# Adding the second mixture's results in the output rows by accumulating scatters, instead of a last pass over two tables

## The chip, the cores and the metric

The kernel runs on one core of a Trainium2 chip. The metric is the device time of the whole kernel in microseconds (us), as a median over runs. PE is the matrix engine (TensorE), ACT ScalarE, DVE VectorE, POOL GpSimd, SP SyncE. SP and ACT issue plain transfers (DMAs); POOL issues indirect ones, which take a list of row numbers (gathers and scatters).

## The reference

Four stages follow one another on 6250 rows (nodes) of 256 features, with 100000 edges: a first graph attention, a first mixture of experts (6 experts, the best two for each row), a second graph attention, and a second mixture of experts. Only the last matters here:

```python
def _L1_ffn_ref(x, Wg, bg, W1, b1, W2, b2):
    xf = x.reshape(-1, D)
    gate_logits = xf @ Wg + bg
    top_w, top_i = jax.lax.top_k(gate_logits, TOP_K)
    top_w = jax.nn.softmax(top_w, axis=-1)
    w_dense = jnp.sum(jax.nn.one_hot(top_i, E, dtype=xf.dtype) * top_w[..., None], axis=1)
    out = jnp.zeros_like(xf)
    for e in range(E):
        h = jax.nn.gelu(xf @ W1[e] + b1[e], approximate=False)
        out = out + w_dense[:, e:e + 1] * (h @ W2[e] + b2[e])
    return out.reshape(B, L, D)
...
x = x + _L1_ffn_ref(_layernorm(x, axis=-1)[None], ...)[0]
```

Each row of the result is the row itself plus the weighted results of two of the eight experts (TOP_K = 2). The hidden size of an expert is 1024.

## The kernel before, in words

Rows are handled in tiles of 128 (NT = 49 tiles, the last one with 106 rows). The class Routed does the bookkeeping of a mixture. For every tile it chooses two experts per row, counts, and gives each (row, expert) pair a slot in a table in DRAM that is grouped by expert (f_rows). POOL scatters the rows there (L768). Whenever 256 slots of one expert are full, they make a block (NB = 256, NTB = 2 tiles of 128). The second mixture plans for 54 blocks. A short block is filled with null rows, whose row numbers lie beyond the last tile.

The function ffn1 (L1421) is the second mixture, interleaved with the second graph attention. Its order of work is written by hand: one loop over steps s (L1520), whose body issues instructions for all five engines, and each engine follows its own queue in that order. seq is the list of the tiles still to be gathered. In a step

- SP loads the next block: its rows xr, its bias columns and its output bias (fetch, L838), the first weights w1 (1 MB, L1453), and for the block before it the second weights w2 (1 MB, fetch2, L1460);
- PE runs the second layer of the block before the last (outer, L1481) and the first layer of the last one (inner, L1470). ACT applies the activation (L1474) and scales the results into buffers named by (L892, four of them, which is two blocks); DVE adds the bias and, for a row's first expert, the row itself (L897, L899);
- POOL gathers the neighbours' rows of one tile for the attention (L1239), with the scatters of the mixture set between the gathers through a list named outbox (L1605). When no gathers are left, the scatters follow one another, each behind a small memset named gap (L1617).

Where a block's result goes: places (L867) works out for each of its rows a row number in a table in DRAM, f1_parts (L640), which has two halves. The first half takes the result of a row's second expert, the other half (at offset part) that of its first; null rows go to places of their own. So every row of the table is written once, and the scatters (send, L902) are declared free of order among each other. While gathers remain (s < len(seq) - 1), the finished blocks aren't scattered at once: SP stores them in a table late_y (L1562). From step len(seq) + 2 on, two of these kept blocks per step are loaded again (fetch_kept, L1513, 256 KB each, three buffers named late) and scattered after the step's own block (L1567-1570). 32 blocks are kept, 22 are scattered directly.

After the loop, rest (L1665) has a loop for blocks that the plan left out; its bounds come from left_i, and for these inputs it has no turn. Then a last pass (L1632-1663) loads both halves of the table, four tiles at a time, on two queues, adds them on DVE (L1658) and stores the sums to the output.

Of the kernel before, what the change touches and what calls it, by code (L numbers as in the profile page):

```python
# [9 lines left out]
F32 = mybir.dt.float32  # L10
# [25 lines left out]
def gnn_moe_kernel(ctx: ExitStack, tc: tile.TileContext, a: dict, out: bass.AP):  # L36
# [587 lines left out]
    class Routed:  # L624
# [4 lines left out]

        def __init__(self, name, n_e, keep_pool, ids, own=False, spare=None):  # L630
            self.name, self.n_e, self.ids, self.own = name, n_e, ids, own
# [6 lines left out]
            self.written_by = []  # L638
            self.part = NT * P + self.n_blocks * NB
            self.parts = dram.tile([2 * self.part, D], F32, name=f"{name}_parts")  # L640
            self.table = dram.tile([n_e * REG + NB, RW], F32, name=f"{name}_rows")
# [225 lines left out]
        def places(self, pool, xr, bcol, j, tok=None):  # L867

            w = pool.tile([P, NTB], F32, name="bw", bufs=4)
            first = pool.tile([P, NTB], F32, name="bfirst", bufs=4)  # L870
            nc.vector.tensor_scalar(first, xr[:, :, C_E0], bcol[:, self.n_c : self.n_c + 1], None, op0=OP.is_equal)
            nc.vector.tensor_mul(w, xr[:, :, C_WD], first)
            nc.vector.tensor_add(w, w, xr[:, :, C_W1])
            if tok is None:
                tok = pool.tile([P, NTB], I32, name="btok", bufs=6)

            off = pool.tile([P, NTB], F32, name="boff", bufs=4)
            nc.vector.tensor_scalar(off, xr[:, :, C_TOK], float(NT * P), float(j * NB), op0=OP.is_ge, op1=OP.mult)
            nc.vector.tensor_add(off, off, xr[:, :, C_TOK])
            nc.vector.scalar_tensor_tensor(tok, first, float(self.part), off, op0=OP.mult, op1=OP.add)  # L880
            return w, tok, first

        def put(self, pool, b, i, py):


            y = self.drawn(pool, b, i, py)
            self.finish(b, i, y)
            return y, b["tok"][:, i : i + 1]

# [11 lines left out]

        def send(self, y, tok):  # L902
            put = nc.gpsimd.indirect_dma_start(  # L903
# [3 lines left out]
            self.apart(put, "parts")  # L907
            tc.add_to_no_dep_group(f"{self.name}parts", put.ins)

        def due(self, n_rows, last):  # L910
# [14 lines left out]
        def left(self, out_i):  # L925

            s = self.short

            nc.vector.tensor_scalar(s[0:1, 0:1], s[0:1, 0:1], -float(self.planned), float(self.planned),
                                    op0=OP.mult, op1=OP.add)  # L930
            nc.vector.tensor_tensor(s[0:1, 1:2], s[0:1, 1:2], s[0:1, 0:1], OP.max)
            nc.vector.tensor_copy(out_i, s)

# [28 lines left out]
    def ffn0(k0, t0_d, a0_d, late, order_pool):  # L962
        NX = a["L0_ffn_expert_w1"].shape[0]
        moe, rw1, rw2, rb1, rb2 = (k0[k] for k in ("moe", "rw1", "rw2", "rb1", "rb2"))
        with tc.tile_pool(name="f0g", bufs=1) as fp, tc.tile_pool(name="f0r", bufs=2) as rp, \
                tc.tile_pool(name="f0w", bufs=4) as wp, tc.tile_pool(name="f0h", bufs=2) as hp, \
                tc.tile_pool(name="g0b", bufs=2) as gp:
            with tc.tile_pool(name="f0p", bufs=2, space=PSUM) as psum:
# [103 lines left out]
                while s < len(pairs) or ready or coming or new or q1 or q2 or q3 or g1 or g2 or g3 or drawn \  # L1072
# [3 lines left out]
                    for b, i, y in drawn:  # L1076
                        moe.finish(b, i, y)
                        results.append(partial(moe.send, y, b["tok"][:, i : i + 1]))
                    drawn = []
# [341 lines left out]
    def ffn1(tab, bias_b):  # L1421
        NX, _, HD = a["L1_ffn_W1"].shape
        NM = HD // P
        with tc.tile_pool(name="f1", bufs=1) as fp, tc.tile_pool(name="f1r", bufs=2) as rp, \
# [9 lines left out]
            list_i = keep.tile([1, 2, P], I32, name="list_i")  # L1434
            left_i = keep.tile([1, 2], I32, name="left_i")
            moe = Routed("f1", NX, fp, node_s, own=True, spare=6 * (NB - 1))
            moe.columns(b1c)
            with tc.tile_pool(name="f1p", bufs=2, space=PSUM) as psum:
# [73 lines left out]

                def fetch_kept(j):  # L1513
                    y = hp.tile([P, NTB, D], F32, name="late", bufs=3)
                    nc.sync.dma_start(y, y_d[j * P : (j + 1) * P])
                    return [partial(moe.send, y[:, i, :], toks[:, j, i : i + 1]) for i in range(NTB)]

                gap = fp.tile([1, 1], F32, name="gap")
                s = 0
                while s < len(seq) or ready or new or cur or prev or q1 or q2 or group or outbox or coming or kept:  # L1520

                    prev, cur = cur, new
                    new = fetch(*ready.pop(0)) if ready else None
                    if cur is not None:
# [33 lines left out]
                    if prev is not None:  # L1558
# [7 lines left out]
                        prev = None  # L1566
                    if s > len(seq) + 1:  # L1567
                        for _ in range(2):
                            if kept:
                                sends += fetch_kept(kept.pop(0))  # L1570
                    if new is not None:
# [59 lines left out]

        with tc.tile_pool(name="f1o", bufs=8) as op_, \  # L1632
                tc.manual_schedule(engines={ET.SP, ET.PE, ET.Activation, ET.DVE, ET.Pool}):
            loads = [(g, min(4, NT - g)) for g in range(0, NT, 4)]
            ys = []

            def load():
                if not loads:
                    return
                g, n = loads.pop(0)  # L1640
                y = op_.tile([P, 2, 4, D], F32, name="yg")
                k = min(n, NFULL - g)
                for c in range(2):
                    r = c * moe.part + g * P
                    eng = nc.sync if c == 0 else nc.scalar
                    if k:
                        eng.dma_start(y[:, c, :k, :], moe.parts[r : r + k * P, :].rearrange("(t p) d -> p t d", p=P))
                    if k < n:
                        eng.dma_start(y[:NTAIL, c, k, :], moe.parts[r + k * P : r + k * P + NTAIL, :])
                ys.append((g, n, k, y))  # L1650

            for _ in range(6):
                load()
            while ys:
                g, n, k, y = ys.pop(0)
                eng = nc.sync if g % 8 else nc.scalar
                if k:
                    nc.vector.tensor_add(y[:, 0, :k, :], y[:, 0, :k, :], y[:, 1, :k, :])  # L1658
                    eng.dma_start(out[g * P : (g + k) * P, :].rearrange("(t p) d -> p t d", p=P), y[:, 0, :k, :])
                if k < n:  # L1660
                    nc.vector.tensor_add(y[:NTAIL, 0, k, :], y[:NTAIL, 0, k, :], y[:NTAIL, 1, k, :])
                    eng.dma_start(out[NFULL * P : N, :], y[:NTAIL, 0, k, :])
                load()

    def rest(moe, list_i, left_i):  # L1665
# [3 lines left out]
        with tc.tile_pool(name="rs", bufs=1) as pool, tc.tile_pool(name="rsp", bufs=1, space=PSUM) as psum:  # L1669
            first = nc.values_load(left_i[0:1, 0:1], min_val=0, max_val=moe.n_blocks)  # L1670
            end = nc.values_load(left_i[0:1, 1:2], min_val=0, max_val=moe.n_blocks)
            with tc.For_i(first, end, 1) as j:
                e = nc.values_load(list_i[0:1, 0, bass.ds(j, 1)], engines=[ET.SP], min_val=0, max_val=NX - 1)
# [18 lines left out]
                tok = pool.tile([P, NTB], I32, name="tok")  # L1692
                nc.vector.scalar_tensor_tensor(tok, first_, float(moe.part), xr[:, :, C_TOK],
                                               op0=OP.mult, op1=OP.add)
                xT = pool.tile([P, 2, NB], F32, name="xT")
# [15 lines left out]
                for i in range(NTB):  # L1711
                    py = psum.tile([P, D], F32, name="py")
                    for m in range(NM):
# [6 lines left out]
                                                   op0=OP.mult, op1=OP.add)  # L1720
                    nc.gpsimd.indirect_dma_start(
                        out=moe.parts[:, :], out_offset=bass.IndirectOffsetOnAxis(ap=tok[:, i : i + 1], axis=0),
                        in_=y, in_offset=None)

# [45 lines left out]
```

## Time and profile before

| | |
|---|---|
| median of 3 runs | 2446.48 us (2446.15 to 2448.04) |
| the profiled execution's own time | 2447.71 us |
| its span (first to last instruction) | 2446.0 us |
| granted PE clock, mean over the span | 0.873 |
| PE busy | 1848.9 us, 76% of the span |
| POOL busy | 1498.5 us, 61% |
| DVE busy, ACT busy | 1222.0 us (50%), 943.2 us (39%) |
| bytes moved | 471.68 MB, 193 GB/s in the mean |
| scatters to f1_parts from late, from by | 64 and 44 |

The page's second part cuts the span into 40 slices of 61.2 us; a digit is the busy share of an engine in a slice, in tenths. A chain of waits follows the work that ended last back to what released it, step by step. A line of a timeline gives the start, the busy time, the engine, the source line, the operation with what it writes and reads, and in brackets the idle time before it with what ended that. "To landing" is the time from the issue of a transfer to the signal that its data has arrived. All source lines in this part of the text are those of the kernel before.

### The profile page before, as it was taken

Reading aid. Unit: us, or ns where it says so; the run is one execution under the profiler, and the core shown is the slowest. Engines: PE = TensorE matmul, PEld = TensorE weight load, DVE = VectorE, ACT = ScalarE, POOL = GpSimd, SP = SyncE. Lnnn points to the kernel's source line nnn. Section 1 sums busy time; section 2 is a strip of 40 time slices with the busy share of each in tenths; the row PEclk is TensorE's granted clock in tenths of the full one; section 3 lists DMA queues with packets and bytes.
Section 4 is the critical chain, followed back from the end, with each engine's and each line's share of the span. In section 5 each row is a group of like instructions: output and inputs, shape, how many; then the busy total and the mean of one; then the engine's idle time right before and its main releaser. Section 6 shows DMA issues by size and latency. Waiting matters only on the chain.

```text
span 2446.0 us, 31094 instructions
## 1 busy us (share of the span) xinstructions
PE 1848.9 (76%) x8343; PEld 1545.0 (63%) x8344; DVE 1222.0 (50%) x4459; ACT 943.2 (39%) x1967; POOL 1498.5 (61%) x1778
## 2 busy tenths in 40 slices
PE   3834757887986455259699999999989797799990
PEld 2622546676774343247588888887778676588880
DVE  3658765653227545365555565655645454311112
ACT  2754445553445421014244444433433332334330
POOL 2556366767637377777777777777777774244420
PEclk8955778998998876679899999999999898899995
DMA  7513354768769644446667767676666665387748
GB/s 215 125 42 118 107 161 134 220 191 243 232 196 299 182 116 109 109 155 188 189 197 245 244 209 243 204 226 222 204 199 204 200 198 157 123 295 258 277 163 314
DMA packets 346251, 471.68 MB, mean 193 GB/s; under 512 B 70205, under 2 KB 283236, under 8 KB 346070
## 3 DMA queue, kind: packets, MB, share of 16 engines
q1 hardware_dynamic: 261868, 272.15, 35.6%
q0 software_dynamic: 72112, 186.44, 25.6%
q10 hardware_dynamic: 12090, 11.03, 1.3%
q8 instruction: 69, 1.13, 0.2%
q14 instruction: 112, 0.92, 0.1%
HBM read 374.44 MB, written 95.02 MB: 192 GB/s over the span
## 4 chain that ended last, share of the span: by engine, by line
PE 38%; POOL 16%; DMA 10%; issue 9%; DVE 7%; ACT 7%; SPq 1%; POOLq 0%; DVEq 0%; ACTq 0%
PE py L1481 10%; PE ph L1470 10%; POOL g L1239 10%; PE sums L1293 7%; PE ph L1038 5%; DMA g<-t_d,idx 4%; POOL f_rows L768 2%; PE py L1048 2%; POOL idx L253 2%; DMA yg<-f_parts 2%; DMA idx<-src_d,start_i 2%; DVE g L1284 1%; ACT L1474 1%; ACT L402 1%; POOL f_parts L903 1%
## 5 line engine op out<-in xcount | busy, mean ns | idle before, releaser
L1239 POOL DMA_INDIRECT g<-t_d,idx x813 | 776.7, 955 | 249.2 <-issue 229.5
L1470 PE MATMUL ph<-bxT,w 128*128 128x256 f32 x1728 | 411.7, 396 | 29.6 <-ACT hT L1474 29.6
L1470 PEld LDWEIGHTS ph<-bxT,w 128*128 128x128 f32 x1728 | 338.2, 199 | 90.5 <-ACT hT L1474 43.0
L1293 PE MATMUL sums<-g,ident 128*128 128x256 f32 x1626 | 386.5, 397 | 3.1 <-DVE g L1284 3.0
L1481 PE MATMUL py<-w,hT 128*128 128x256 f32 x1728 | 384.9, 381 | 0.3 <-DMA w<-in_L_ffn_W 0.3
L1293 PEld LDWEIGHTS sums<-g,ident 128*128 128x128 f32 x1626 | 323.1, 200 | 59.9 <-DVE g L1284 12.5
L1481 PEld LDWEIGHTS py<-w,hT 128*128 128x128 f32 x1728 | 328.3, 191 | 45.1 <-DMA w<-in_L_ffn_W 0.5
L768 POOL DMA_INDIRECT f_rows<-rw,slot x196 | 199.4, 1017 | 91.8 <-issue 45.9
L897 DVE SCALAR_TENSOR_TENSOR by<-ob,bw,by 128x256 f32<-128x256 f32 x216 | 98.0, 481 | 266.9 <-ACT by L892 266.9
L1474 ACT ACTIVATE hT<-ph,bcol 128x256 f32<-128x256 f32 x432 | 177.9, 472 | 137.5 <-PE ph L1470 132.2
L1284 DVE TENSOR_TENSOR g<-g,weights 128x2048 f32<-128x2048 f32 (+6 forms) x88 | 229.6, 2610 | 0.0
L903 POOL DMA_INDIRECT f_parts<-by,btok x108 | 105.5, 977 | 153.1 <-DVE by L897 105.3
L1263 ACT ACT_TABLE_LOAD x36 | 46.2, 1283 | 391.7 <-DVE lg L1262 268.3
L1550 PE MATMUL pT<-ident,xn 128*128 128x128 f32 x98 | 24.5, 341 | 184.8 <-DVE xn L1547 184.8
L892 ACT ACTIVATE by<-py,bw 128x256 f32<-128x256 f32 x216 | 92.5, 473 | 154.9 <-PE py L1481 121.8
L1041 ACT ACTIVATE h<-ph,bcol 128x256 f32<-128x256 f32 x216 | 90.7, 471 | 158.6 <-PE ph L1038 97.8
L903 POOL DMA_INDIRECT f_parts<-by,toks x44 | 42.3, 961 | 161.8 <-DVE by L899 123.2
L1550 PEld LDWEIGHTS pT<-ident,xn 128*128 128x128 f32 x98 | 13.4, 167 | 197.5 <-issue 188.7
L1254 DVE TENSOR_TENSOR lg<-g,own 128x32 f32<-128x32 f32 (+6 forms) x88 | 16.7, 199 | 238.3 <-DMA g<-t_d,idx 211.2
L446 PE MATMUL proj<-we,xT 128*128 128x264 f32 x392 | 107.7, 421 | 27.5 <-ACT xT L462 27.5
L1038 PE MATMUL ph<-bxT,w 128*128 128x256 f32 x432 | 110.6, 412 | 16.0 <-ACT bxT L864 14.9
L1038 PE MATMUL ph<-h,w 128*128 128x256 f32 x432 | 112.8, 420 | 0.6 <-ACT h L1041 0.6
(325 smaller groups left out, 2909.7 us busy)
## 6 DMA issues: line engine op xcount, KB each, us to landing
w<-in_L_ffn_W SPq DMA_DIRECT2D x108, 1024.0 KB
w<-in_L_ffn_expert_w SPq DMA_DIRECT2D x162, 256.0 KB
xr<-f_rows SPq DMA_DIRECT2D x108, 264.0 KB
yg<-f_parts SPq DMA_DIRECT2D x36, 512.0 KB
g<-t_d,idx POOLq DMA_INDIRECT x813, 3.2
late_y<-by SPq DMA_DIRECT2D x64, 128.0 KB
late<-late_y SPq DMA_DIRECT2D x32, 256.0 KB
ob<-in_L_ffn_expert_b SPq DMA_DIRECT2D x54, 128.0 KB
```

The lines of the kernel that those rows point to most:

```text
L446: nc.tensor.matmul(ph, xT[:, k, :], we[:, k, :], start=(k == 0), stop=(k == 1))
L768: put = nc.gpsimd.indirect_dma_start(out=self.table[:, :], out_offset=bass.IndirectOffsetOnAxis(ap=slot[:np_, c, i : i + 1], axis=0), in_= ...
L892: nc.scalar.activation(y, py, AF.Copy, scale=b["w"][:, i : i + 1])
L897: nc.vector.scalar_tensor_tensor(y, b["ob"], w, y, op0=OP.mult, op1=OP.add)
L903: put = nc.gpsimd.indirect_dma_start(out=self.parts[:, :], out_offset=bass.IndirectOffsetOnAxis(ap=tok, axis=0), in_=y, in_offset=None,)
L1038: nc.tensor.matmul(ph[:, m, :], b["ws"][i][:, k, m * P : (m + 1) * P], hi[:, k, :], start=(k == 0), stop=(k == 1))
L1239: nc.gpsimd.indirect_dma_start(out=g[:, k, :], out_offset=None, in_=halves(tab), in_offset=bass.IndirectOffsetOnAxis(ap=idx[:, o : o + 1], ...
L1284: nc.vector.tensor_mul(gv, gv, al[:, k0 : k0 + m, :, None].to_broadcast([P, m, H, C]))
L1293: nc.tensor.matmul(po, ident, g[:, k, :D], start=False, stop=k0 + k == q["K"] - 1)
L1470: nc.tensor.matmul(ph[:, q, :], b["w1"][:, k, m * P : (m + 1) * P], b["xT"][:, k, :], start=(k == 0), stop=(k == 1))
L1474: nc.scalar.activation(hT[:, m, :], ph[:, q, :], AF.Gelu, bias=b["bcol"][:, m : m + 1])
L1481: nc.tensor.matmul(py, b["hT"][:, m, i * P : (i + 1) * P], b["w2"][:, m, :], start=(m == 0), stop=(m == NM - 1))
```

## The change

The second mixture gets the output itself as its table (argument result). The row numbers are the plain ones, and each scatter adds to the output row in place of writing to a row of its own. Null rows have numbers above the last row and are dropped by a bounds check. The output must be zero before the first addition, so SP writes zeros to it, seven tiles at a time, in the first seven steps of ffn1 (clear). Scatters of one block name different rows and are declared free of order among each other; scatters of different blocks are not, so the first of a block waits until those of the block before have landed. Kept blocks are fetched from step len(seq) on, in one load of two blocks, into the buffers of the gathers (g, five of them), and they are scattered ahead of the step's own block. The last pass is removed. rest gets a further loop, with zero or one turn, that clears the output again when the plan was broken. In the changed file the lines of ffn1 and of the steps before it lie up to 32 lines lower; the scatter is L924, the ACT copy into by L897.

```diff
-        def __init__(self, name, n_e, keep_pool, ids, own=False, spare=None):
+        def __init__(self, name, n_e, keep_pool, ids, result=None, own=False, spare=None):
+            self.result = result
...
+            if self.result is not None:
+                nc.vector.tensor_copy(tok, xr[:, :, C_TOK])
+                return w, tok, first
...
-        def send(self, y, tok):
+        def send(self, y, tok, j):
+            if self.result is not None:
+                put = self.added(y, tok)
+                tc.declare_no_dep(put.ins, group=f"{self.name}sum{j}", reason="other rows")
+                tc.add_to_no_dep_group(f"{self.name}sum{j}", put.ins)
+                return
...
+        def added(self, y, tok):
+            return nc.gpsimd.indirect_dma_start(
+                out=self.result[:, :], out_offset=bass.IndirectOffsetOnAxis(ap=tok, axis=0),
+                in_=y, in_offset=None, bounds_check=self.result.shape[0] - 1, oob_is_err=False, compute_op=OP.add,
+            )
...
+    def clear(rows, zero, g, n):
+        k = min(n, rows.shape[0] // P - g)
+        nc.sync.dma_start(rows[g * P : (g + k) * P, :].rearrange("(t p) d -> p t d", p=P),
+                          zero[:, None, :].to_broadcast([P, k, D]))
+        if k < n:
+            nc.sync.dma_start(rows[NFULL * P : N, :], zero[:NTAIL, :])
...
-            moe = Routed("f1", NX, fp, node_s, own=True, spare=6 * (NB - 1))
+            moe = Routed("f1", NX, fp, node_s, out, own=True, spare=6 * (NB - 1))
...
-                def fetch_kept(j):
-                    y = hp.tile([P, NTB, D], F32, name="late", bufs=3)
-                    nc.sync.dma_start(y, y_d[j * P : (j + 1) * P])
-                    return [partial(moe.send, y[:, i, :], toks[:, j, i : i + 1]) for i in range(NTB)]
+                def fetch_kept(js):
+                    g = ap_.tile([P, CH, D + H], F32, name="g", bufs=5)
+                    y = g.rearrange("p k d -> p (k d)")[:, : len(js) * NTB * D].rearrange(
+                        "p (b i d) -> p b i d", i=NTB, d=D)
+                    nc.sync.dma_start(y, y_d[js[0] * P : (js[-1] + 1) * P].rearrange("(b p) i d -> p b i d", p=P))
+                    return [partial(moe.send, y[:, b, i, :], toks[:, j, i : i + 1], j)
+                            for b, j in enumerate(js) for i in range(NTB)]
...
+                    if s < NT // 7:
+                        clear(out, moe.null[:, 0, :D], s * 7, 7)
...
-                    if s > len(seq) + 1:
-                        for _ in range(2):
-                            if kept:
-                                sends += fetch_kept(kept.pop(0))
+                    if s >= len(seq) and kept:
+                        sends = fetch_kept(kept[:2]) + sends
+                        del kept[:2]
...
-        with tc.tile_pool(name="f1o", bufs=8) as op_, \
...
-                if k:
-                    nc.vector.tensor_add(y[:, 0, :k, :], y[:, 0, :k, :], y[:, 1, :k, :])
-                    eng.dma_start(out[g * P : (g + k) * P, :].rearrange("(t p) d -> p t d", p=P), y[:, 0, :k, :])
...
+            again = nc.values_load(left_i[0:1, 2:3], min_val=0, max_val=1)
+            zero = pool.tile([P, D], F32, name="zero_rows")
+            nc.vector.memset(zero, 0.0)
+            with tc.For_i(0, again, 1):
+                for g in range(0, NT, 7):
+                    clear(moe.result, zero, g, 7)
```

More of the change, by code (lines that the diff above doesn't have):

```diff
@@ L638, in __init__ @@
             self.written_by = []
-            self.part = NT * P + self.n_blocks * NB
-            self.parts = dram.tile([2 * self.part, D], F32, name=f"{name}_parts")
+            if result is None:
+                self.part = NT * P + self.n_blocks * NB
+                self.parts = dram.tile([2 * self.part, D], F32, name=f"{name}_parts")
             self.table = dram.tile([n_e * REG + NB, RW], F32, name=f"{name}_rows")
@@ L887, in put @@
             self.finish(b, i, y)
-            return y, b["tok"][:, i : i + 1]
+            return y, b["tok"][:, i : i + 1], b["j"]
         def drawn(self, pool, b, i, py):
@@ L927, in left @@
             s = self.short
+            nc.vector.tensor_copy(out_i[:, 2:3], s[0:1, 0:1])
             nc.vector.tensor_scalar(s[0:1, 0:1], s[0:1, 0:1], -float(self.planned), float(self.planned),
@@ L931, in left @@
             nc.vector.tensor_tensor(s[0:1, 1:2], s[0:1, 1:2], s[0:1, 0:1], OP.max)
-            nc.vector.tensor_copy(out_i, s)
+            nc.vector.tensor_copy(out_i[:, 0:2], s)
+    def clear(rows, zero, g, n):
[4 more added lines that the diff above has]
+            nc.sync.dma_start(rows[NFULL * P : N, :], zero[:NTAIL, :])
     def prepare0(fp, k):
@@ L1077, in ffn0 @@
                         moe.finish(b, i, y)
-                        results.append(partial(moe.send, y, b["tok"][:, i : i + 1]))
+                        results.append(partial(moe.send, y, b["tok"][:, i : i + 1], b["j"]))
                     drawn = []
@@ L1434, in ffn1 @@
             list_i = keep.tile([1, 2, P], I32, name="list_i")
-            left_i = keep.tile([1, 2], I32, name="left_i")
-            moe = Routed("f1", NX, fp, node_s, own=True, spare=6 * (NB - 1))
+            left_i = keep.tile([1, 3], I32, name="left_i")
+            moe = Routed("f1", NX, fp, node_s, out, own=True, spare=6 * (NB - 1))
             moe.columns(b1c)
@@ L1630, in ffn1 @@
         rest(moe, list_i, left_i)
-        with tc.tile_pool(name="f1o", bufs=8) as op_, \
[L1633 to L1645, printed above, removed]
-                    if k:
[L1647 to L1657, printed above, removed]
-                    nc.vector.tensor_add(y[:, 0, :k, :], y[:, 0, :k, :], y[:, 1, :k, :])
-                    eng.dma_start(out[g * P : (g + k) * P, :].rearrange("(t p) d -> p t d", p=P), y[:, 0, :k, :])
[L1660 to L1663, printed above, removed]
     def rest(moe, list_i, left_i):
@@ L1692, in rest @@
                 tok = pool.tile([P, NTB], I32, name="tok")
-                nc.vector.scalar_tensor_tensor(tok, first_, float(moe.part), xr[:, :, C_TOK],
-                                               op0=OP.mult, op1=OP.add)
+                nc.vector.tensor_copy(tok, xr[:, :, C_TOK])
                 xT = pool.tile([P, 2, NB], F32, name="xT")
@@ L1720, in rest @@
                                                    op0=OP.mult, op1=OP.add)
-                    nc.gpsimd.indirect_dma_start(
-                        out=moe.parts[:, :], out_offset=bass.IndirectOffsetOnAxis(ap=tok[:, i : i + 1], axis=0),
-                        in_=y, in_offset=None)
+                    moe.added(y, tok[:, i : i + 1])
     with tc.tile_pool(name="order", bufs=1) as order_pool, \
```

## The prediction

> **What bounds the kernel now.** I read the slices of the page first, then the end of the chain of waits, then POOL's timeline in the last stage, then the landings of the transfers and the DMA share inside one step.
>
> The page's rows in 40 slices of 61.2 us, for the two engines and the DMA that matter:
>
> ```profile
> PE   3834757887986455259699999999989797799990
> POOL 2556366767637377777777777777777774244420
> DMA  7513354768769644446667767676666665387748
> ```
>
> Up to slice 34 POOL (gathers) and PE share the second mixture's work. From slice 35 (about 2140 us) PE alone is full, and in the last slice it stands still. The end of the chain, in order of time (start, us, what):
>
> ```profile
> 2367.07 6.91 PE ph L1470 x32
> 2373.98 6.92 PE py L1481 x32
> ...
> 2382.71 3.32 DMA f_parts<-by,toks
> ...
> 2386.79 5.25 DMA yg<-f_parts
> 2392.06 11.28 DMA yg<-f_parts
> 2403.36 10.87 DMA yg<-f_parts
> ...
> 2414.31 11.09 DMA out<-yg
> ...
> 2425.42 12.38 DMA yg<-f_parts
> ...
> 2437.92 0.43 DVE yg L1661
> ```
>
> So two stages set the end. From 2146 us, blocks of 256 rows pass PE at 14.25 us each (two runs of 32 matmuls, 6.91 us each, and 0.35 of transposes) until 2380.9. Then comes the last pass, 2386.8 to the end at 2446.0, bound by DMA. In the block stage POOL has room: its timeline over one step is
>
> ```profile
> 2194.42 0.96 POOL L903 DMA_INDIRECT f_parts<-by,toks  x1 [4.69 <-DVE by L899]
> ...
> 2197.87 0.95 POOL L903 DMA_INDIRECT f_parts<-by,toks  x1 [2.41 <-DVE bfirst L871]
> ...
> 2199.13 0.96 POOL L903 DMA_INDIRECT f_parts<-late,toks  x1 [0.22 <-issue]
> ...
> 2202.92 0.96 POOL L903 DMA_INDIRECT f_parts<-late,toks  x1 [0.22 <-issue]
> ```
>
> Six scatters per step (two of the fresh block, four of two kept blocks), one every 1.27 us, none waiting for another. Their landings, from issue, first those from late, then those from by (2180 to 2360 us):
>
> ```profile
> DMA to landing us min/median/max: 2.4/2.4/2.8
> ```
> ```profile
> DMA to landing us min/median/max: 5.4/5.6/5.7
> ```
>
> The difference is the state of the DMA engines. Busy times and, at the end, clock, DMA share and GB/s, in two parts of one step:
>
> ```profile
> 2217.00:2227.00 10.00, 10.00 (x50) 8.82 (x49) 2.71 (x10) 3.88 (x9) 2.73 (x5) 1.00 0.94 315
> 2227.00:2231.50 4.50, 4.50 (x23) 3.94 (x22) 0.10 (x1) 1.89 (x6) 3.62 (x9) 1.00 0.44 151
> ```
>
> Each step has a burst of about 10 us (two weight loads of 1 MB, the rows, the late rows) and a quiet rest. A scatter issued in the burst lands after 5.6 us, one in the quiet part after 2.4. Today nobody waits for that.
>
> **What goes.** The whole last pass (L1632-1663: 24 loads of 512 KB, 13 adds, the stores). The scatter issued at 2382.71 has landed by about 2385.1; the exit of the loop in rest (L1672) takes until 2386.9. In the changed program there are two such loops, 2 x 1.8 = 3.6 us, then POOL's closing drain (4.65 us in the trace, covered today by the last pass) and about 1.0 us of closing as at the end here: 9.3 us (5 if the drain is shorter). A kernel that kept today's block stage would end at 2385.1 + 9.3 = 2394.4, which is 51.6 us earlier. Also gone are 3 DVE instructions of 0.16 us per block in places (54 blocks); DVE is busy 45.5 of 236 us in this stage, so nothing.
>
> **What is added, off the path.** The seven clears write 6.4 MB from SP at the start of ffn1. They have no wait in front of them, and SP waits 230 us for the first list of blocks there (SPq L836), so nothing is queued behind them. POOL's gathers run there at one per 1.25 us whether or not they land late, at a DMA share of 0.40. 0 to 5 us, below nothing excluded since nothing is taken away; I take 1. Without that idle stretch they would cost 6.4 MB at about 300 GB/s, 21 us. The kept rows are loaded in one issue of 512 KB instead of two of 256, two steps earlier; on SP they keep their place behind the load of w2 and ahead of the next block's rows (they took SP 2.0 us per step there, between waits for PE), and they reuse the gather buffers, five deep, so SP waits only if POOL falls four steps behind: nothing. The scatter now also checks its indices; every indirect DMA in the trace takes POOL 0.94 to 1.02 us in the mean whatever it moves, so nothing, up to a few tenths per scatter, which the range has room for.
>
> **What is added on the path: the wait.** In the changed program's order on POOL the first scatter of every block waits for the landing of both scatters of the block before it; within a block they go together. Queued behind that wait on POOL are the next blocks' scatters; behind those waits ACT, which refills by (4 buffers, two blocks), and so PE (py has 2). Nothing here is hidden by gathers, since they are over.
>
> One block then takes 1.27 us (second issue) + landing + 0.2 us (POOL's gap between instructions). What is not in the trace is the landing of an accumulating scatter, which must read the row in HBM before it writes it.
> - Quiet, lower bound: 2.4 us as a plain scatter (a gain is excluded: it moves no less). Upper: a gather (which reads HBM, at least 2.7) and then a scatter (2.4), 5.15. The two share the making of the descriptors, about 1.5 us from issue (2382.71) to the first packets (the DMA slices show them from 2384.1), so I take 5.15 - 1.5 = 3.65. Block: 5.1 us.
> - Burst: a plain scatter loses 5.6 - 2.4 = 3.2 us before its turn. Lower bound 5.6 (as plain). If the read of the target and the write each wait for one turn it is 3.65 + 6.4 = 10.05; with one turn 6.85. I take two turns, as the row that it is nearest to (a gather followed by a scatter, each with its turn). Block: 11.5 us.
>
> A step of 14.25 us needs three blocks while kept ones remain. With one block in the burst and two in the quiet part, S = 11.5 + 2 x 5.1 = 21.7 us. POOL becomes the bound.
>
> [...] No run here shows an accumulating DMA. [...]
>
> **The sum.** 54 blocks: 22 fresh, 32 kept in 16 pairs. The first fresh five come at 2046, 2058, 2086, 2107 and 2131, far enough apart for the first four pairs. From 2147.5, where POOL's late rows are there as now, twelve triples (a pair and a fresh block) remain: 12 S. After that blocks 18 and 19 are ready, and PE has stood before block 20: half a first layer 3.6, five runs of about 7.1 (35.5), ACT, DVE and issue 4, landing 3.65, together 47. End = 2147.5 + 12 S + 47 + 9.3 + 1 (clears) = 2204.8 + 12 S. With S = 21.7: 2465 us. Against this execution's span of 2446.0 that is +19; the execution took 2447.7 with what lies around the span, the median of the three runs is 2446.5, so I add 1 and say 2466. The formula meets today's span at S = 20.1 us, a mean of 6.7 us per block. It has a floor of 2395, where PE stays the bound.
>
> **Rivals.**
> 1. Faster: an add needs one turn in the burst only. [...] Against it: read and write of HBM are two dependent steps. It decides below a mean of 6.7 us per block. That the waits do not take place (the change not doing what it says) would give 2395 too; the order on POOL shows them, so that has hardly a chance.
> 2. Much slower: every row of an add is a packet of its own, eight per DMA engine, with a turn each. Then quiet landings are at the upper end (block 6.6) and a block in the burst lasts the burst out, 13: S = 26.2, end 2519. For it: nothing in this trace separates rows; against it: 128 rows go as 32 packets of 4 KB today.
> 3. No change: the last pass only reappears as waits, S 19.7 to 20.5.
>
> **Chances.** Forecast (2451 to 2490) 0.44; rival 1 0.36; rival 2 0.11; rival 3 0.09. What a measurement can tell from no change is about 0.2%, 5 us: faster 0.36, same 0.09, slower 0.55. The range takes in rival 1 down to the rule's 2402 and leaves out the floor and rival 2: 2402 to 2495. The likeliest case's own range is 2451 to 2490.
>
> **What would show it.** Right: no loads of yg; first scatters of a block on POOL idle before "DMA out"; quiet landings near 3.7, landings in the burst near 10; steps of 21 to 22 us from 2150 with PE idle behind ACT by L897; the last scatter about 12 us before the end. Wrong: landings near 3 or burst landings near 6 with PE full at 14.25 us per step (rival 1), landings above 5 in the quiet part (rival 2), or clears that push the gathers' stage back by more than 5 us.

## The result, and the profile after

The changed kernel took 2505.41 us (median of 4 runs, 2499.81 to 2506.27) beside 2446.32 us for the kernel before on the same chip: 1.0244 times as long, 95% interval 1.0226 to 1.0261. Its profiled execution took 2499.81 us with a span of 2498.0 us, 52 us more than the span of before. The experiments below ran on four chips on which the last gather started 785 to 886 us later (at 2897.5 us for the changed kernel, against 2036.9 here; the cause is open). So their times stand as ratios to the kernel before on the same chip (3314 to 3373 us there), and the part after the last gather is read from the traces. That part is longer there too: 478.9 us for the changed kernel, against 461.2 here.

The slices of the changed kernel's page (62.5 us each), as shown of before, with the row of the granted PE clock added:

```profile
PE   4743757797967363569799999899898877877777
POOL 3557447767555577677777777777777765244443
PEclk8955969998989776779899999999999988988888
DMA  7514346677879743364776776767676656866752
```

The last pass is gone (no slice in which PE reads 0), but in the last five slices PE reads 7 where it read 9 until the last pass, and its clock 8 where it read 9. POOL reads 4, hardly more than before: it stands more than it works. POOL's timeline over one triple (two kept blocks, a fresh one, and the start of the next triple), the counterpart of the step shown before:

```profile
2190.91 1.76 POOL L924 DMA_INDIRECT out<-g,toks  x1 [2.88 <-issue]
...
2192.97 1.56 POOL L924 DMA_INDIRECT out<-g,toks  x1 [0.27 <-issue]
...
2197.63 1.55 POOL L924 DMA_INDIRECT out<-g,toks  x1 [3.06 <-DMA out<-g,toks]
...
2199.49 1.56 POOL L924 DMA_INDIRECT out<-g,toks  x1 [0.27 <-issue]
...
2206.83 1.55 POOL L924 DMA_INDIRECT out<-by,toks  x1 [5.74 <-DMA out<-g,toks]
...
2213.20 1.65 POOL L924 DMA_INDIRECT out<-g,toks  x1 [2.90 <-issue]
```

The first scatter of a block stands behind "DMA out" for about 3 us in the quiet part and 5.7 us in the burst of this triple (some of these waits are put down to issue). The scatter itself is recorded with 1.56 us where it took 0.96, and the second one follows after 1.87 us, not 1.27. The waits of all engines from 2140 us to the end (sum, times, longest):

```profile
DVE by L902 <- ACT by L897: 307.6, 29, 21.4
ACT by L897 <- DMA out<-by,toks: 162.4, 26, 14.5
POOL out L924 <- DMA out<-g,toks: 118.2, 25, 8.5
...
PE ph L1498 <- ACT hT L1502: 74.8, 13, 8.1
```

Read from below, this is the chain that was forecast: PE waits for ACT, ACT for by, and by for the landing of a scatter that stands behind others on POOL. The same stretch of work in windows (busy times, then clock, DMA share, GB/s), first the changed kernel over twelve triples, then the kernel before over fourteen of its steps:

```profile
2159.86:2435.45 275.59, 204.37 (x833) 171.67 (x832) 31.72 (x96) 66.44 (x156) 116.72 (x144) 0.87 0.67 167
```
```profile
2180.40:2380.00 199.60, 199.60 (x952) 175.77 (x951) 38.40 (x134) 79.22 (x179) 79.97 (x153) 1.00 0.71 242
```

A PE step, from fresh block to fresh block, takes 23.0 us instead of 14.26, and PE isn't full. Its own work has become longer as well: a block is 68 matmuls, so 833 of them are 12.25 blocks, 16.7 us each at a granted clock of 0.87, against 14.26 at 1.00. In one step this can be seen in place: PE waited 5.9 us, until 2192.48, and the granted clock is 0.50 in the window around the restart, while it is 1.00 in the stretches before (2185.0 to 2191.8) and after (2198.8 to 2212.0):

```profile
2191.90:2198.60 6.70, 6.12 (x14) 4.88 (x15) 0.66 (x4) 2.09 (x6) 3.37 (x6) 0.50 0.37 42
```

How an addition moves is told by the page's row for the queue of the indirect DMAs (packets, MB, share), before and after:

```profile
q0 software_dynamic: 72112, 186.44, 25.6%
```
```profile
q0 software_dynamic: 82480, 185.10, 27.7%
```

There are 10368 packets more for 108 scatters, 96 each, with no more bytes. A plain scatter goes as 32 packets of 4 KB, an adding one as 128 packets of 1 KB, as many as it has rows (from 2382 to 2387 us the kernel before moves its one scatter in 32 packets of 2 to 8 KB; from 2193.1 to 2197.5 us the changed kernel moves a block's two in 256 of 512 B to 2 KB). By the landing signals in the trace, the quiet scatter issued at 2192.97 has landed at 2196.87 (3.9 us), the one issued in the burst at 2199.49 at 2206.09 (6.6 us), and the next block's scatter starts 0.76 and 0.74 us after them.

### The profile page after: what moved, and what is told of

Same layout as the page of the kernel before. It is cut to its first block, busy times and chain, and to the rows that moved or that the text cites. A ratio compares the mean times of both kernels' runs of the same rounds, so it can differ in the third digit from the quotient of the medians.

```text
span 2498.0 us, 31088 instructions
## 1 busy us (share of the span) xinstructions
PE 1878.7 (75%) x8343; PEld 1564.8 (63%) x8344; DVE 1193.0 (48%) x4340; ACT 939.9 (38%) x1967; POOL 1560.8 (62%) x1778
## 3 DMA queue, kind: packets, MB, share of 16 engines
q0 software_dynamic: 82480, 185.10, 27.7%
HBM read 361.64 MB, written 95.02 MB: 183 GB/s over the span
## 4 chain that ended last, share of the span: by engine, by line
## 5 line engine op out<-in xcount | busy, mean ns | idle before, releaser
L1498 PE MATMUL ph<-bxT,w 128*128 128x256 f32 x1728 | 446.9, 418 | 104.2 <-ACT hT L1502 104.1
L1498 PEld LDWEIGHTS ph<-bxT,w 128*128 128x128 f32 x1728 | 360.2, 213 | 178.3 <-ACT hT L1502 122.9
L897 ACT ACTIVATE by<-py,bw 128x256 f32<-128x256 f32 x216 | 92.3, 473 | 245.2 <-DMA out<-by,toks 162.4
L924 POOL DMA_INDIRECT out<-g,toks x64 | 101.8, 1591 | 128.9 <-DMA out<-g,toks 53.0
L924 POOL DMA_INDIRECT out<-by,toks x44 | 69.0, 1568 | 134.1 <-DMA out<-g,toks 83.7
L1066 PE MATMUL ph<-bxT,w 128*128 128x256 f32 x432 | 106.5, 401 | 14.5 <-ACT bxT L866 13.2
```

The lines of the kernel that those rows point to most:

```text
L924: return nc.gpsimd.indirect_dma_start(out=self.result[:, :], out_offset=bass.IndirectOffsetOnAxis(ap=tok, axis=0), in_=y, in_offset=None, ...
L1066: nc.tensor.matmul(ph[:, m, :], b["ws"][i][:, k, m * P : (m + 1) * P], hi[:, k, :], start=(k == 0), stop=(k == 1))
L1498: nc.tensor.matmul(ph[:, q, :], b["w1"][:, k, m * P : (m + 1) * P], b["xT"][:, k, :], start=(k == 0), stop=(k == 1))
```

## The experiments

Main theory A: the addition makes each scatter dearer (longer issue, row by row, longer landing), and only the wait between blocks brings that into the time. Rivals: W, the order of the blocks alone costs it; C, the bounds check is what lengthens the issue; D, the additions slow other transfers even where nobody waits. Besides these, the late start of the triples (L), the loads as the cause of the burst (e4), and the place of the kept blocks ahead of the fresh one (B) were tried.

| run | ratio to the kernel before (95%) | part after the last gather, us |
|---|---|---|
| kernel before, first chip | 1 | 402.4 |
| changed kernel, first chip | 1.0244 (1.0226 to 1.0261) | 461.2 |
| c_after, the changed kernel | 1.0153 (1.0129 to 1.0176) | 478.9 |
| e1 waits without addition | 0.9936 (0.9912 to 0.9959) | 415.5 |
| e5 the same again | 0.9974 (0.9963 to 0.9985) | 417.3 |
| e2 addition without waits | 0.9989 (0.9973 to 1.0005) | 428.6 |
| e6 the same again | 1.0000 (0.9990 to 1.0011) | 427.5 |
| e3 four kept blocks early | 1.0096 (1.0067 to 1.0125) | 470.8 |
| e4 no weight loads late | 1.0050 (1.0030 to 1.0070) | 456.1 |
| e8 fresh block first | 1.0031 (1.0018 to 1.0044) | 444.3 |
| e7 22 blocks kept | 0.9881 (0.9864 to 0.9899) | 403.4 |
| e9 the same again | 0.9825 (0.9801 to 0.9849) | 405.0 |
| e10 16 blocks kept | 0.9766 (0.9750 to 0.9782) | 388.3 |
| e11 8 blocks kept | 0.9646 (0.9626 to 0.9666) | 375.7 |

On one chip each ran e1 to e4; c_after, e5, e6 and e7; e8 to e10; and e11. A comparison of whole times across chips goes by ratios, and is less sure than the intervals say: the same kernel differs by 0.4% of the kernel before between e1 and e5, and by 0.6% between e7 and e9. The kernel before has no profile on these chips; e6, which takes its time, stands for it.

**c_after.** The changed kernel, unaltered.

> The changed kernel as it is, as the measure for the others of this group on the same chip. 1.024 times the kernel before, three blocks in 22.97 us in the last stage.

Measured: slower again, by 1.5% of a longer time, or 51 us (59 us in the first result). The twelve triples, counted from fresh block to fresh block, take 22.4 us each there (23.0 in the first profile).

**e1 and e5, waits without addition.** In added:

```diff
-                in_=y, in_offset=None, bounds_check=self.result.shape[0] - 1, oob_is_err=False, compute_op=OP.add,
+                in_=y, in_offset=None, bounds_check=self.result.shape[0] - 1, oob_is_err=False,
```

> The changed kernel with plain scatters to the output rows: the waits, the clears and the bounds check stay, only the addition is left out (so each output row holds the result of one expert alone). Theory A, the addition makes the scatter dearer and with it every wait: the scatter takes POOL 0.96 us again, lands after 2.4 us quiet and 5.6 us in the burst, so a block takes 1.27 + 2.4 + 0.75 = 4.4 us (quiet) or 7.6 us (burst), three blocks 16.4 us instead of 22.97, and the kernel 2505 - 12 x 6.6 = 2426 us (2410 to 2435), faster than before. Rival W, the order of the blocks alone costs it whatever the scatter does: 2495 to 2505 us. Rival C, it is the bounds check that makes the issue long: POOL still takes 1.56 us for a scatter, three blocks 16.4 + 6 x 0.6 / 2 = 18.2 us, 2448 us.

> The kernel of e1 again (waits without the addition), in a group with the changed kernel itself. Its last stage took 17.5 us for three blocks in e1. Theory A, the addition costs 5.5 us for three blocks: 12 x 5.5 = 66 us below the changed kernel, about 2505 - 66 = 2440 us, and 2425 to 2445 with the shorter tail; ratio to the kernel before 0.990 to 1.000. Rival W, the waits alone: as the changed kernel, 1.02.

Measured: 63 us below the changed kernel in e5's group (3315.56 against 3378.55), and 61.6 us of it after the last gather. The scatters of e5 from 3000 us to the end (count, busy, mean ns, idle before), and its queue of indirect DMAs:

```profile
L924 POOL DMA_INDIRECT out<-g,toks x52 | 53.0, 1020 | 118.4 <-issue 48.2 <-DMA out<-g,toks 32.6 <-DMA g<-late_y 25.0
L924 POOL DMA_INDIRECT out<-by,toks x36 | 35.2, 978 | 89.3 <-DMA out<-g,toks 46.4 <-DVE by L904 23.9 <-issue 10.0
```
```profile
q0 software_dynamic: 72112, 185.09, 19.2%
```

With the bounds check still in place the issue is back at about 0.98 us and the packets at their number of before, so C falls: issue and packets belong to the addition. Between two kept blocks of a triple 4.6 us pass (median) instead of 6.6 in c_after, and a triple takes 18.1 us instead of 22.4, so twelve triples account for 52 of the 63 us. W falls as the whole cause. It holds for a part: with waits alone the kernel is only 0.3 to 0.6% below the kernel before, and its part after the last gather only 10 us shorter than e6's, although the last pass, put at 51.6 us in the forecast, is gone.

**e2 and e6, addition without waits.** The kernel before, its scatters adding to rows of their own:

```diff
-            self.part = NT * P + self.n_blocks * NB
+            self.part = NT * P if own else NT * P + self.n_blocks * NB
...
-                in_=y, in_offset=None,
+                in_=y, in_offset=None,
+                **(dict(bounds_check=2 * NT * P - 1, oob_is_err=False, compute_op=OP.add) if self.own else {}),
```

Null rows go beyond the table, and SP clears its two halves in the first seven steps.

> The kernel before with accumulating scatters into its own table of two halves, cleared in the first steps of ffn1 (12.8 MB); every row has its own place, so no block waits for another, and the last pass stays. Theory A, an addition costs only where somebody waits for it: six scatters of 1.87 us are 11.2 us of POOL in a step of 14.25 us, PE stays the bound, 2446 us plus 0 to 5 for the clears (2444 to 2452). Rival D, the 128 packets of each addition slow the other transfers or POOL falls behind: a step is longer than 14.25 us, by 1 us or more in 22 steps, 2468 us or more.

> The kernel of e2 again (additions to rows of their own, without waits, the last pass stays), in a group with the changed kernel itself. Theory A: an addition costs nothing where nobody waits for it, 1.000 to 1.003 times the kernel before (2444 to 2454 us). Rival D, its 128 packets and the longer issue slow the stage: 1.009 or more.

Measured: no difference from the kernel before in either. The scatters in e6's last part:

```profile
L904 POOL DMA_INDIRECT f_parts<-late,toks x64 | 100.3, 1567 | 61.8 <-DMA late<-late_y 46.8 <-issue 15.0
L904 POOL DMA_INDIRECT f_parts<-by,toks x44 | 69.2, 1572 | 99.4 <-DVE by L900 80.7 <-DVE bfirst L871 11.2 <-issue 4.0
```

They are as long as in the changed kernel, and none waits for "DMA f_parts". A window of this stage (columns as before):

```profile
3044.00:3232.00 188.00, 186.94 (x890) 164.17 (x889) 37.35 (x130) 74.90 (x169) 124.97 (x157) 1.00 1.02 263
```

PE is 99% busy and passes a block in 14.4 us. The addition costs no time where POOL has room and nobody waits; D falls. But it does occupy the DMA engines: their share is 1.02 here (the times of packets that overlap are added up), against 0.71 in the kernel before on the first chip, at nearly the same pace of PE. POOL's waits for kept rows are longer too (46.8 us, against 18.9 in the last stage before). So an addition isn't shown to be free for other transfers; it only delayed nobody who sets the end.

**e3, four kept blocks early.**

```diff
-                        sends = fetch_kept(kept[:2]) + sends
-                        del kept[:2]
+                        n_k = 4 if s < len(seq) + 2 else 2
+                        sends = fetch_kept(kept[:n_k]) + sends
+                        del kept[:n_k]
```

> The changed kernel with its first two loads of kept results taking four blocks each instead of two, so that POOL has blocks to scatter while SP waits for the last rows (POOL stood 19 us there at 2123 to 2142 us, and 13.5 us before its first kept block). Theory L, the late start of the triples is a term of its own, 17 to 21 us: the chain on POOL ends earlier by what POOL no longer stands, 2505 - 15 to 25 = 2480 to 2490 us. Rival: the early blocks of the pairs collide with by and hold PE, nothing is gained, 2500 to 2510 us.

Measured: 0.57% below c_after's ratio, some 19 us of 3360, with an interval of about 12 us either way; but the two ran on different chips, between which one and the same kernel differed by as much (e7 and e9). After the last gather the profiles differ by 8 us only. The last kept block goes 38 us earlier (371.7 against 409.5 us after the last gather), but the last scatter only 8 us earlier (458.8 against 466.8). The end of e3's timeline on POOL shows why:

```profile
3364.61 1.56 POOL L924 DMA_INDIRECT out<-by,toks  x1 [9.20 <-DVE by L904]
...
3378.43 1.55 POOL L924 DMA_INDIRECT out<-by,toks  x1 [8.76 <-DVE by L904]
```

After the kept blocks POOL waits 9 us for DVE at each fresh block: PE still has the blocks to do that it was held up from, at 14 us each. L gets little support: the earlier start gains 8 us by the profiles, and most of its time goes to the blocks that PE has left.

**e4, no weight loads in the last stage.** From block 36 on, w1 and w2 are those loaded for an earlier block.

```diff
-                    w1 = wp.tile([P, 2, HD], F32, name="w1")
...
+                    if j < 36:
+                        w1 = wp.tile([P, 2, HD], F32, name="w1")
...
+                        held["w1"] = w1
+                    w1 = held["w1"]
...
+                    if b["j"] >= 36:
+                        b["w2"] = held["w2"]
+                        return
```

> The changed kernel in which blocks from number 36 on use the weights of an earlier block that are still in place (so their results are those of other weights): no loads of w1 and w2 in the last stage. Theory A with one turn in the burst: without the loads every block lands as the quiet ones do, three blocks take 3 x 6.5 = 19.5 us instead of 22.97, 2505 - 12 x 3.4 = 2464 us (2455 to 2472). Rival N, landings of an addition are long by themselves and the loads do not matter: 2500 to 2506 us.

Measured: 1.0% below c_after's ratio (35 us), of which 23 us after the last gather; but the triples take 21.5 us (22.4 in c_after), not 19.5. One block per triple is still late, now the second kept one:

```profile
3114.35 1.56 POOL L924 DMA_INDIRECT out<-g,toks  x1 [5.91 <-DMA out<-g,toks]
...
3120.72 1.55 POOL L924 DMA_INDIRECT out<-by,toks  x1 [2.91 <-DMA out<-g,toks]
```

That block takes 8.8 us in the mean, where one in the burst takes 9.8 in c_after: the burst is weaker but not gone. What is left in that burst are the kept rows (512 KB), the next block's rows (264 KB) and its output bias (128 KB). So neither expectation held: the weight loads, 2 of the 2.9 MB of a burst, make a small part of its price, 0.9 us per triple or 11 us in all. Which of the other loads makes a block late is open, and so is the rest of the gain.

**e8, the fresh block first.** The same 32 kept blocks, behind the step's own block, one per step.

```diff
+                    prev_ys = prev is not None
...
-                        sends = fetch_kept(kept[:2]) + sends
-                        del kept[:2]
+                        n_k = 4 if s < len(seq) + 2 else 1 if prev_ys else 2
+                        sends += fetch_kept(kept[:n_k])
+                        del kept[:n_k]
```

> The changed kernel with the same 32 kept blocks, but scattered behind the step's own block instead of ahead of it, one per step (four in each of the first two loads, two per step once no fresh block is left). Theory B, the kept blocks that go ahead of the fresh one hold up by, ACT and PE, and PE's blocks after the last kept one are what ends late: with one kept block a step takes 16.7 us (a block in the burst and a quiet one), PE ends with the scatters, the part after the last gather is 20 to 35 us shorter than that of the changed kernel: 0.8 to 1.4% of the kernel before less than the changed kernel has. Rival P, POOL's sum of 54 blocks sets the end whatever the order: within 0.3% of the changed kernel.

Measured: 1.2% below c_after's ratio and 34.6 us less after the last gather, with the same number of additions and waits. Windows of each while PE has blocks to do, c_after first (window, busy times of PE, its loads, DVE, ACT and POOL, clock, DMA share, GB/s):

```profile
3067.00:3294.00 227.00, 169.01 (x690) 141.99 (x689) 26.21 (x80) 55.37 (x130) 97.42 (x121) 0.86 0.68 171
```
```profile
3045.00:3290.00 245.00, 234.72 (x1101) 203.80 (x1101) 40.75 (x124) 88.83 (x205) 100.28 (x124) 0.99 0.76 208
```

PE goes from 74% to 96% busy and from a clock of 0.86 to 0.99. B holds: a triple in one PE step wastes PE, and a double (a kept and a fresh block, 16.2 us here) wastes little. PE's last matmul ends at 3292.1 us, 70 us before the end; what ends last now is the chain on POOL, with kept blocks 6.4 us apart after the last fresh one.

**e7 and e9 to e11, fewer kept blocks.** The first 10, 16 or 24 blocks are scattered between the gathers; the rest are kept. For e7 and e9 (e10 and e11 have 16 and 24 in place of 10):

```diff
-                        if s < len(seq) - 1:
+                        if s < len(seq) - 1 and prev["j"] >= 10:
...
-                        sends = fetch_kept(kept[:2]) + sends
-                        del kept[:2]
+                        n_k = 4 if s < len(seq) + 2 else 1
+                        sends = fetch_kept(kept[:n_k]) + sends
+                        del kept[:n_k]
```

> The changed kernel in which the first ten blocks are scattered at once between the gathers (where the landing is hidden by gathers), and only 22 are kept: two loads of four, then one kept block per step. If a block costs 7.66 us of POOL in the last stage and 2 x 1.87 us between gathers, the chain on POOL ends at 2068 + 10 x 3.74 + 44 x 7.66 = 2442 us and PE at 2394 + 37 + 5 = 2436: about 2442 us (2432 to 2460), 60 us below the changed kernel and 0 to 0.5% below the kernel before. Rival: the scatters between the gathers wait there too, or PE loses blocks: 2470 us or more.

> The kernel of e7 again (ten blocks scattered between the gathers, 22 kept). If POOL sets the pace of the gathers on this chip, as in the first profiles, ten blocks cost 10 x 3.74 = 37 us there and the part after the last gather is 60 to 75 us shorter than in the changed kernel: 2465 us against 2446 to 2505, between the two, ratio 1.003 to 1.012. If something else paces the gathers, as it did in e7, they cost nothing there and the ratio is 0.986 to 0.991 as in e7.

> As e9 with 16 blocks scattered between the gathers and 16 kept. Six doubles less on the last stage, where a double takes 16.7 us and PE alone 14.25: 6 x 2.5 = 15 us less there, 6 x 3.74 = 22 us more in the gathers if POOL paces them. So 7 us above e9 if POOL paces the gathers, 15 us below e9 (about 0.983 to 0.986) if it doesn't.

> As e10 with 24 blocks scattered between the gathers and 8 kept, which all go in the first two loads. The eight doubles of the last stage that are left in e10 (16.6 us a step against PE's 14.25) go too: 8 x 2.4 = 19 us less after the last gather, 388 to 369 us. If POOL doesn't pace the gathers, as in all runs of this study so far: ratio 0.977 - 0.006 = 0.971 (0.968 to 0.975). If POOL paces them, 8 x 3.74 = 30 us more there, and the kernel is slower than e10 by 10 us.

Measured: each is faster than the kernel before, by 1.2 and 1.8%, 2.3% and 3.5%, and with that more than any of the expectations had it. Between the gathers no scatter waits for a landing (in e10 POOL stands 7.6 us in 25 short gaps and 5.0 us for DVE before its 32 scatters there). The part after the last gather shrinks about as expected (403, 388, then 376 us against 369 expected); the rest of the gain lies ahead of it. e11's last stage is PE's again:

```profile
2970.00:3180.00 210.00, 210.00 (x1002) 184.93 (x1001) 35.72 (x114) 84.50 (x191) 46.51 (x60) 1.00 0.60 176
```

PE is busy all the time at full clock, 14.25 us per block. e11's gathers ended 75 us earlier than c_after's, on another chip; e7's ended 22 us earlier on the same one. Why they do is open: in the runs of this study something other than POOL paced the gathers (537 us of POOL's waits in c_after are for PE's sums, which the first profile hardly has). In the first profiles POOL's gathers follow one another with gaps of 0.3 us, and a block scattered between the gathers would cost an estimated 2 x 1.87 = 3.74 us there. Whether these versions beat the kernel before on that chip has not been measured. By that price they would be below the changed kernel by 75 - 37 = 38 us (e7), 91 - 60 = 31 (e10) and 103 - 90 = 13 (e11), all short of the 59 us that it lies above the kernel before.

## Why the prediction was wrong

The side (slower) and the mechanism (POOL's waits for landings, behind them ACT and PE) were right, the size was not: 2466 us was forecast, 39 us below the median, and the range ended at 2495. The profile splits the miss. Twelve triples and what follows them gave a span of 2465 by the sum, and 2498 was measured:

| term | forecast | measured | difference, us |
|---|---|---|---|
| start of the twelve triples | 2147.5 | 2168.8 | +21.3 |
| 12 S, from pair to pair | 12 x 21.7 | 12 x 22.67 | +11.6 |
| from there to the end | 57.3 | 57.2 | -0.1 |

The other 6 us are between the profiled execution (2499.81) and the median.

**The step that failed first: the loads of kept rows put at nothing since "on SP they keep their place", and with it "far enough apart for the first four pairs".** The forecast let the first four pairs pass between the early fresh blocks. Three did. SP's longest wait before the fourth pair, and its queue from 2110 us on:

```profile
SPq L786 <- DVE ci L805: 27.7, 1, 27.7
```
```profile
2115.77 9.67 SPq L788 DMA_DIRECT2D f_rows<-null  x8
2128.73 0.40 SPq L846 DMA_DIRECT2D xr<-f_rows  x1
...
2132.27 0.47 SPq L1545 DMA_DIRECT2D g<-late_y  x1
```

and POOL:

```profile
2142.42 1.61 POOL L924 DMA_INDIRECT out<-g,toks  x1 [19.04 <-DMA g<-late_y]
...
2152.24 1.56 POOL L924 DMA_INDIRECT out<-g,toks  x1 [6.27 <-DMA out<-g,toks]
...
2159.86 1.55 POOL L924 DMA_INDIRECT out<-by,toks  x1 [4.16 <-DMA out<-g,toks]
```

The fourth pair's load stands on SP behind a wait of 27.7 us for the last counts, eight fills with null rows, and the next block's rows and weights; POOL starts 10 us after its issue. So POOL stood 19 us, and the fresh block behind that pair went at 2159.86, where the kernel before sends it at 2131. A load that nobody waited for was counted as free although its consumers now stand ahead of the fresh block. The +21.3 us is its place in this sum, not what a repair would give back: e3 started earlier and gained 8 us after the last gather, since PE was still held up by the kept blocks.

**S, mis-sized in three places that partly cancel, so that its small error is in part luck.** A quiet block was put at 1.27 + 3.65 + 0.2 = 5.1 us. Between two kept blocks it is 1.87 + 3.9 + 0.75 = 6.5: the landing was well bounded (its 3.65 was put together from a gather, a scatter and an estimated 1.5 us that the two would share; no run shows that sharing), but "every indirect DMA in the trace takes POOL 0.94 to 1.02 us" says nothing of an adding one (+0.6, more than the few tenths that were allowed for), and POOL's gap of 0.2 us between instructions is not the time from a landing to the next start (+0.55). The other quiet one, from the fresh block to the next pair, takes 6.0 in the mean. Together they are 2.3 us more than was put. The block in the burst was put at 11.5 us with two turns of 3.2. It takes 10.1 in the mean: the landing of 3.9 became 6.6 us in the triple above and 7.1 in the median of the twelve, 2.7 to 3.2 us more, which is the 3.2 once and not twice. "Turn" is the forecast's name for these 3.2 us, by which the scatters of before landed later in the burst (5.6 against 2.4); that transfers take turns is not shown by any run. So "I take two turns" was wrong and rival 1 right on that point, which gave 1.4 us back. What the delay comes from is open: without the weight loads the late block was only 1.0 us faster (e4). The point from which rival 1 decides, a mean of 6.7 us per block, holds for the forecast's start; with the measured start and end of the triples it is (2446 - 2168.8 - 57.2) / 36 = 6.1. The measured 22.67 / 3 = 7.6 is on the slow side of both, and e5 with 18.1 / 3 = 6.0 ended near the kernel before, as this would have it.

**Rival 2** was right that every row is a packet of its own (128 packets of 1 KB) and wrong on what that costs: it had a landing of 5.15 us in the quiet part and a block of 13 in the burst, and 3.9 and 10.1 were measured. **The lower end of the range, 2402,** stands for S = (2402 - 2204.8) / 12 = 16.4; no run shows a rule that gives it. Measured was 22.67. e5, without any addition, already has 18.1, and the addition brings 4.3 more: between two kept blocks a plain scatter's block takes 4.6 us and an adding one's 6.6 (e5 and c_after). That an addition reads its target first is what adding means; as a transfer of its own the read shows in no count: the pages have 361.64 MB read from HBM after and 374.44 before, less by the 12.8 MB of the last pass, and the queue of the indirect DMAs moves 185.10 MB with the addition and 185.09 without it (e5). What does show is the share of the DMA engines, 1.02 in e6 against 0.71.

**What held:** the last pass is gone, and the close takes as long as put (from the last landing, 2488.7, to 2498.0: 9.3 us, as forecast). The clears show nowhere: the last gather starts at 2036.9 us, against 2043.6 before. ACT behind by, and PE behind ACT, were the chain that was named. The prediction didn't ask what standing does to PE: a block of PE work takes 16.7 us in a stage where PE waits. With S at 22.67 that is still hidden, but it leaves PE less room to make up for a wait.

## What to carry to other kernels

An order between transfers cost here, for each link, the issue, the whole landing and the restart, 6.0 to 6.5 us quiet and 10 in a burst. This price is to be read per link against the step of the engine that bounds the stage: two links (16.2 us in e8) overran PE's 14.25 us a little and three (22.4 in c_after) by far. The same additions cost no time without a wait (ratios of 0.9989 and 1.0000 in e2 and e6), and with other work between the links their waits were gone (e7 to e11, on chips where POOL had time to spare there); so before adding such an order, ask which work can stand between two links, and put the links there. When a load's consumer is moved ahead of others in a queue, price everything that stands ahead of that load.

## What the runs showed of the hardware

- An adding indirect scatter of 128 rows of 1 KB is recorded on POOL with 1.56 us instead of 0.98 (the next one starts after 1.87 instead of 1.27), goes as 128 packets instead of 32, and lands after 3.9 us in the quiet part instead of 2.4. The bounds check alone changes none of the issue (0.97 to 0.98 us in the median in e5) and the packets (72112 in e1 and e5). The record of the small memset behind each scatter begins about 0.97 us after the scatter's start in both cases (1.18 at the longest in the triple shown) and lasts 0.61 us instead of 0.09, so the profile doesn't tell which of the two the extra 0.6 us belongs to.
- From a landing to the start of the waiting scatter on POOL 0.74 to 0.78 us pass in most links of the changed kernel's triples, 0.27 in six.
- With additions and no waits the DMA engines' share was 1.02 (e6), against 0.71 in the kernel before.
- PE's granted clock was lower in the stages in which PE worked with pauses: 1.00 in e11's and before's steady stage, 0.99 in e8, 0.87 in the changed kernel, with PE busy all of the time, 96% and 74% of it. The pauses are in front of the first layer (from 2140 us on 13 waits for ACT, 5.8 us in the mean, 8.1 the longest), and its matmuls took 451 ns in the mean there, those of the second layer 379. The clock is 0.50 around the end of the 5.9 us wait shown above and 1.00 before and after it. How long a pause must be for that is not shown.
- On the experiments' chips ACT stood in front of the copy into xT (L1585) for 427.5 us in 24 waits in c_after, released by something that the profile doesn't name. In the first profiles that wait is 162.3 us and ends with PE. Its cause is open.
